# Order of the first loads and of two VectorE forks in a fused attention and feed-forward kernel on one core

## Chip, cores and metric

The kernel runs on one core of one Trainium2 chip. The metric is the device time of one execution in microseconds (us), median of several runs. Before the change the four runs took 618.7 to 620.2 us, median 619.73.

## What is computed

The input x has 8 sequences of 1024 tokens and 256 channels. It is normalized over the channels (layer norm without weights), and two branches are added to it. Cut to what matters:

```python
xn = layernorm(x)                                  # (8, 1024, 256)
# branch 1: a gated linear recurrence ("hawk"), 384 wide
gate = xn @ Wg.T;  u = xn @ Wi.T
y = depthwise_causal_conv(u, conv_w, 4 taps) + conv_b
ig = sigmoid(y @ lru_Wi.T + lru_bi);  rg = sigmoid(y @ lru_Wg.T + lru_bg)
alpha = exp(-8 * softplus(lam) * rg);  beta = sqrt(1 - alpha**2 + 1e-6)
h = scan(h[t] = alpha[t] * h[t-1] + beta * ig * y)
branch1 = (gelu(gate) * h) @ Wo.T
# branch 2: a feed-forward part with token shift
xr, xk = mu * xn + (1 - mu) * xn_shifted_by_one_token
branch2 = sigmoid(xr @ W_r.T) * (relu(xk @ W_k.T)**2 @ W_v.T)
out = x + branch1 + branch2
```

All values are float32.

## The kernel before, in words

One sequence of 1024 tokens is a round; there are eight rounds, named "first", "second", "middle" (five of them) and "last" in the table `PLACES`. Most products work on two row blocks, two column blocks and two halves of 512 tokens at once with seven block products in place of eight: `Group` (L457) writes the steps of such a group out. To that end GpSimd makes sums of weight blocks (`weight_sum`, L396, once per weight in the first round) and sums of tokens (`token_sum`, L794, in each round; the add itself is L803). Inside a group, ScalarE copies one bank of PSUM to another (`seed`, L491) and one to SBUF (`five`, L496), and VectorE adds them back in two places: `fork_c` (L499) and `fork_d` (L507). The products that follow a fork write into the banks that the fork reads or writes, so TensorE waits for it. The groups are u (three groups: u and the gate), k, r, v, o and l (three groups: the two LRU gates). TensorE's products stand at L415 (tokens in the free dimension) and L421 (tokens by row).

Instructions are issued in an order that is written out by hand. Every step is put into a list with a time, TensorE's steps with a running count, the others with their own; for the others the table `PLACES` overrides that time by a planned one, relative to the start of the round. The list is sorted by time (L1303) and issued, so each engine gets its instructions in that order and works through them one by one. A time in `PLACES` therefore sets an instruction's place in its engine's queue, and nothing else.

The second round's steps that matter here: `recur 1 R` is the second half of the scan of hidden block 1 (L930), `gated_state` multiplies the gate by the scanned state (L934), `decay_rest` makes 1 - alpha squared out of the square (L915), and `beta` takes the root of that on ScalarE (L918).

The head stands ahead of the list, at L1001 to L1105. SP issues the loads of x's first round, eight tiles of 128 tokens in four DMAs (L707). ScalarE issues the first half of u's weights (`w_i`, the "i" rows of tile `w_u`), the parameters (`par`) and a table load. Then SP issues the other weights (L349): `w_g` (the "g" rows of `w_u`), `w_k`, `w_r`, two halves of `w_l`, `w_v`, `w_o`. DMAs take their completion semaphores in turn out of eight; a DMA that takes one again is not issued before the DMA that had it last has landed. TensorE meanwhile makes 15 products of a zeroed tile (`busy`, L1025) that nobody reads. VectorE takes the statistics of each tile of x (L725, L729), ScalarE the deviation (L732), VectorE its inverse (L739, L740), and ScalarE and VectorE normalize a tile each (L749, L747). TensorE transposes two tiles (L1044), ScalarE copies them to `xnT` (L1057), and quarters of the first u group follow (L581). This repeats for four pairs of tiles. As soon as all of `xnT` is there, the token sums on GpSimd and the first group with sums (u1) can start; GpSimd has the weight sums of u, r and k ahead of the first token sum in its queue.

The lines that the change touches:

Of the kernel before, what the change touches and what calls it, by code (L numbers as in the profile page):

```python
# [9 lines left out]
AF = mybir.ActivationFunctionType  # L10
# [100 lines left out]
        "inverse 0 8": 25.96, "k late": 26.1, "conv_rest 0 1": 26.33, "u2 evict A 0 0": 26.78,  # L111
        "k evict C 0 1": 27.46, "u2 fork_c": 27.83, "gated_state 2": 28.63, "k evict B 1 0": 29.25,
        "recur 1 L": 30.04, "r seed": 31.03, "u2 fork_d": 31.49, "token_sum v 0": 31.49,
        "r five": 31.72, "u1 evict B 1 0": 32.4, "recur 1 R": 32.66, "normalize 0 1": 33.08,
        "token_sum v 1": 34.07, "r fork_c": 34.27, "r evict A 0 0": 34.3, "normalize 4 1": 34.34,
        "u2 evict C 0 1": 34.87, "gated_state 1": 34.95, "u2 evict B 1 0": 35.51, "conv_first 2": 36.19,
        "token_sum v 2": 36.35, "r fork_d": 36.36, "conv_rest 0 2": 37.5, "normalize 3 1": 37.52,
        "normalize 1 1": 38.22, "v seed": 38.92, "token_sum o 1": 38.98, "v five": 39.6,
# [21 lines left out]
        "l0 evict D 1 1": 72.36, "stats 2 1": 72.76, "token_sum k 1": 73.26, "decay 1": 73.3,  # L140
        "stats 5 1": 73.49, "stats 3 1": 74.22, "token_sum k 2": 74.42, "l2 seed": 74.64,
        "stats 1 1": 74.95, "l2 five": 75.33, "token_sum k 3": 75.59, "l1 fork_d": 75.68,
        "decay_square 1": 76.01, "mix r 1": 76.75, "l1 evict C 0 1": 77.36, "decay_rest 1": 78.25,
        "decay 2": 78.3, "l2 evict A 0 0": 79.64, "l2 fork_c": 80.36, "decay_square 2": 80.44,
        "decay_rest 0": 80.5, "decay_rest 2": 81.72, "l1 evict B 1 0": 82.36, "l1 evict D 1 1": 83.36,
        "l2 fork_d": 84.36, "l2 evict C 0 1": 90.66
    },
# [94 lines left out]
def kernel(  # L242
# [24 lines left out]
    nc = tc.nc  # L267
    B, S, D = x.shape
    TT = S // P
# [6 lines left out]
    def fixed(name, shape, dtype=F32):  # L276
        return const.tile([P] + shape, dtype, tag=name, name=name)


    par = fixed("par", [COLS])  # L280
# [57 lines left out]
    def take():  # L338
        return free.pop(0)

    def give(b):
        free.append(b)
# [4 lines left out]
    def load_weight(engine, name, src):  # L347
        family, first = ROWS[name]
        engine.dma_start(families[family][:, :, first * P : first * P + src.shape[2]], src)  # L349
# [356 lines left out]
    def load(s, t, n):  # L706
        nc.sync.dma_start(  # L707
            xt[:, t : t + n, :],
            x[s, t * P : (t + n) * P, :].rearrange("(t p) d -> p t d", p=P),
        )  # L710
# [8 lines left out]
    def stats(s, t, n):  # L719
        sums_of_tiles(s, t, n)  # L720
        moments(s, t, n)
# [279 lines left out]
    with tc.manual_schedule():  # L1001
# [1 line left out]
        nc.gpsimd.memset(ln_eps, LN_EPS)  # L1003
        nc.gpsimd.memset(beta_eps, BETA_EPS)
        make_identity(nc, ident)
        for t in range(0, TT, 2):
            load(0, t, 2)
            if t == 2:
                load_weight(nc.scalar, "i", w_i)
                nc.scalar.dma_start(par, params)  # L1010
                nc.scalar.preload_act_table(AF.Sqrt)
        load_weight(nc.sync, "g", w_g)
        load_weight(nc.sync, "k", w_k)
        load_weight(nc.sync, "r", w_r)
        load_weight(nc.sync, "lg", lru_wg)
# [6 lines left out]
        def busy(n):  # L1022
            for _ in range(n):
                b = take()
                nc.tensor.matmul(banks[b], warm[:, 0:P], warm, start=True, stop=True)  # L1025
                give(b)
# [40 lines left out]
                mu_rest, par[:, COL_MU_R : COL_MU_K + DC], -1.0, 1.0, ALU.mult, ALU.add  # L1067
            )

        busy(15)  # L1070
        stats(0, 0, 2)
        scales(0, 2)
        early_normalize(0)
# [42 lines left out]
        for s in range(B):  # L1116
# [118 lines left out]
            else:  # L1235
# [36 lines left out]
                L, R = HALVES  # L1272
# [90 lines left out]
```

## Time and profile before

| What | us |
|---|---|
| median of four runs | 619.73 |
| profiled execution, its own time | 619.65 |
| its span, first to last instruction | 617.9 |
| TensorE (PE) busy | 612.0 |
| VectorE (DVE) busy | 532.5 |
| ScalarE (ACT) busy | 472.9 |
| GpSimd (POOL) busy | 320.4 |
| 28 SP loads of x of 256 KB each, median from issue to landing | 5.0 |

The profile is one execution taken by the hardware profiler. Its lines give, in the timelines, start, duration, engine, source line, operation, output and inputs, shapes and count, and in brackets the idle time ahead and what ended it. A line that ends in "x2" merges two instructions in a row. A float32 product shows as two TensorE instructions. In the chain of waits a line gives start, duration and what the time went to. In the DMA view a queue's line gives packets, megabytes and the share of the sixteen DMA engines' time; q1 is SP's queue, q10 is ScalarE's. TensorE is busy in nearly all of the span, so what counts is where it stands still: little things of a few tenths of a microsecond.

### The profile page before, as it was taken

The page shows a single profiled execution, that of the slowest core. Times are in us where ns is not written, and L with a number is a line of the kernel's source. Part 1 is how long each engine was busy: PE and PEld are TensorE (multiplying, and loading weights), DVE is VectorE, ACT ScalarE, POOL GpSimd, SP SyncE. Part 2 cuts the span into 40 slices and gives each one's busy share as a digit, 9 for nine tenths or more (in the row PEclk, how much of TensorE's full clock was granted, in tenths as well). Part 3 has the DMA queues.
Part 4 walks back from the last instruction along what each step waited for, and adds up shares of the span by engine and source line. Part 5 has one row for each costly group of instructions (what it writes and reads, how often), then busy time and mean ns, then how long its engine had stood idle before and what let it go on. Part 6 is the DMA issues. An engine that isn't in the chain of part 4 may idle for free.

```text
span 617.9 us, 7488 instructions
## 1 busy us (share of the span) xinstructions
PE 612.0 (99%) x2539; PEld 369.5 (60%) x2539; DVE 532.5 (86%) x659; ACT 472.9 (77%) x671; POOL 320.4 (52%) x227
## 2 busy tenths in 40 slices
PE   9999999999999999999999999999999999999997
PEld 5475445954469544794448844497445964457466
DVE  5898799999989798898899888998888986789696
ACT  5888998568894788938889398884898749884880
POOL 4977914578044950549307492084911769427000
PEclk9999999999999999999999999999999999999999
DMA  8100600164002810039000480006500044000403
GB/s 282 60 1 10 127 0 1 31 174 69 0 1 50 197 27 0 1 77 198 0 1 1 107 166 1 1 6 154 114 0 1 14 124 69 0 0 1 69 17 119
DMA packets 35478, 35.10 MB, mean 57 GB/s; under 512 B 2800, under 2 KB 34928, under 8 KB 35440
## 3 DMA queue, kind: packets, MB, share of 16 engines
q1 hardware_dynamic: 26416, 25.63, 15.0%
q0 software_dynamic: 8320, 8.39, 9.1%
q10 hardware_dynamic: 704, 0.60, 0.3%
q8 instruction: 20, 0.33, 0.2%
q14 instruction: 18, 0.15, 0.1%
HBM read 19.94 MB, written 8.39 MB: 46 GB/s over the span
## 4 chain that ended last, share of the span: by engine, by line
PE 94%; DVE 2%; POOL 1%; DMA 1%; issue 0%; SPq 0%; DVEq 0%; POOLq 0%
PE bank L415 65%; PE bank L421 25%; PE bank L830 4%; DMA w_u<-in_w_g_dram 1%; POOL sum_u L408 1%; DVE xr L820 1%; POOL xsum L803 0%; DVE bank L499 0%; PE bank L754 0%; SPq L707 0%; DVE q L915 0%; POOL sum_k L408 0%; DVE st L725 0%; POOL sum_r L408 0%; DVE q L930 0%
## 5 line engine op out<-in xcount | busy, mean ns | idle before, releaser
L415 PE MATMUL bank<-y,w_l 128*128 128x512 f32 x288 | 138.2, 593 | 0.1
L898 DVE SCALAR_TENSOR_TENSOR y<-u,par,y 128x1024 f32<-128x1024 f32 x72 | 111.6, 1573 | 0.2
L491 ACT COPY bank<-bank 128x512 f32<-128x512 f32 x76 | 43.7, 576 | 61.3 <-PE bank L415 45.4
L415 PEld LDWEIGHTS bank<-y,w_l 128*128 128x128 f32 x288 | 52.9, 190 | 59.2 <-issue 56.9
L499 DVE TENSOR_TENSOR bank<-bank,five 128x512 f32<-128x512 f32 x76 | 52.3, 689 | 27.4 <-PE bank L415 26.0
L415 PE MATMUL bank<-ysum,sum_l 128*128 128x512 f32 x144 | 71.1, 594 | 0.2
L415 PE MATMUL bank<-xsum,sum_u 128*128 128x512 f32 x138 | 69.5, 593 | 0.8 <-POOL xsum L803 0.8
L803 POOL TENSOR_TENSOR tr<-g 128x512 f32<-128x512 f32 x12 | 22.0, 1837 | 83.7 <-ACT u L611 69.8
L803 POOL TENSOR_TENSOR ysum<-y,ysum 128x512 f32<-128x512 f32 x16 | 28.5, 1782 | 53.6 <-DVE y L898 51.1
L803 POOL TENSOR_TENSOR xsum<-ysum 128x512 f32<-128x512 f32 x12 | 16.0, 1351 | 66.0 <-PE bank L421 58.8
L496 ACT COPY five<-bank 128x512 f32<-128x512 f32 x76 | 43.6, 583 | 5.8 <-PE bank L415 3.8
L415 PEld LDWEIGHTS bank<-ysum,sum_l 128*128 128x128 f32 x144 | 26.8, 190 | 35.3 <-issue 28.7
L415 PE MATMUL bank<-xnT,w_u 128*128 128x512 f32 x92 | 47.0, 592 | 0.0
L415 PEld LDWEIGHTS bank<-xsum,sum_u 128*128 128x128 f32 x138 | 25.6, 190 | 30.8 <-issue 27.0
L623 ACT ACTIVATE tr<-bank,half_b 128x512 f32<-128x512 f32 x48 | 32.0, 679 | 14.7 <-PE bank L415 14.7
L421 PE MATMUL bank<-w_o,g 128*128 128x128 f32 x288 | 37.0, 275 | 0.0
L623 ACT ACTIVATE ti<-bank,half_b 128x512 f32<-128x512 f32 x48 | 31.5, 683 | 7.1 <-PE bank L415 6.9
L421 PEld LDWEIGHTS bank<-w_o,g 128*128 128x128 f32 x288 | 35.0, 192 | 2.9 <-issue 2.9
L749 ACT ACTIVATE xt<-xt,mv,std 128x256 f32<-128x256 f32 x60 | 33.9, 595 | 0.9 <-DVE mv L740 0.9
L922 DVE SCALAR_TENSOR_TENSOR ti<-ti,y 128x1024 f32<-128x1024 f32 (+1 forms) x25 | 29.9, 1216 | 3.9 <-ACT ti L623 3.9
L803 POOL TENSOR_TENSOR ysum<-y 128x512 f32<-128x512 f32 x16 | 20.4, 1276 | 23.8 <-DVE y L898 20.0
L925 DVE SCALAR_TENSOR_TENSOR ti<-ti,q 128x1024 f32<-128x1024 f32 (+1 forms) x25 | 31.8, 1271 | 0.7
(165 smaller groups left out, 1479.3 us busy)
## 6 DMA issues: line engine op xcount, KB each, us to landing
side<-in_x_dram POOLq DMA_DIRECT2D x8, 1024.0 KB, 9.2
xt<-in_x_dram SPq DMA_DIRECT2D x28, 256.0 KB, 5.0
xnT<-xk SPq DMA_DIRECT2D x96, 64.0 KB, 2.0
out_dram<-side SPq DMA_DIRECT2D x12, 512.0 KB, 4.9
xt<-in_x_dram SPq DMA_DIRECT2D x1, 1024.0 KB, 5.3
out_dram<-side SPq DMA_DIRECT2D x4, 256.0 KB, 2.2
out_dram<-side SPq DMA_DIRECT2D x6, 128.0 KB, 1.7
w_l<-in_lru_wg_dram SPq DMA_DIRECT2D x1, 576.0 KB, 5.8
```

What stands on the lines that cost most here:

```text
L415: nc.tensor.matmul(banks[b], weight, tokens, start=start, stop=True, skip_group_check=True)
L421: nc.tensor.matmul(banks[b][:, p], tokens[:, p], weight, start=start and j == 0, stop=True, skip_group_check=True,)
L491: nc.scalar.copy(banks[bank["B"]], banks[bank["A"]])
L496: nc.scalar.copy(self.five, banks[bank["C"]])
L499: nc.vector.tensor_tensor(banks[bank["C"]], banks[bank["B"]], self.five, ALU.add)
L623: nc.scalar.activation(dst[:, m, HALVES[h]], src, AF.Tanh, bias=half_b[:, b + m : b + m + 1], scale=0.5)
L749: nc.scalar.activation(xa, xa, AF.Identity, bias=m, scale=r)
L803: nc.gpsimd.tensor_tensor(dst[o], a, b, ALU.subtract)
L830: nc.tensor.matmul(banks[b][:, j * D : (j + 1) * D], lhs[:, c, (t + j) * P : (t + j + 1) * P], families[w][:, c, :], start=(j == 0 and c = ...
L898: nc.vector.scalar_tensor_tensor(y[:, m, :], u[:, m, k : k + S], column(COL_CONV_W + k * HC + m), y[:, m, :], ALU.mult, ALU.add,)
L922: nc.vector.scalar_tensor_tensor(ti[:, m, p], ti[:, m, p], 1.0, y[:, m, p], ALU.add, ALU.mult)
L925: nc.vector.scalar_tensor_tensor(ti[:, m, p], ti[:, m, p], 0.5, q[:, m, p], ALU.mult, ALU.mult)
```

## The change

It has two parts. In the head, the first two tiles of x are loaded by two DMAs of one tile each in place of one DMA of two; all of u's weights are issued by ScalarE (`w_i`, then `w_g`), ahead of `par` and the table load, while SP goes on from x to `w_k`; and TensorE makes ten warm-up products in place of 15. With one DMA more and the turn of the semaphores changed, SP's issue of `w_k` is now the one that waits for `w_i`; `w_r` waits for the first tile of x.

In the second round two steps change their place in VectorE's queue: `r fork_c` now stands ahead of `recur 1 R`, and `l2 fork_c` ahead of `decay_rest 1`. On the other engines the second round is issued as before.

```diff
 "second" in PLACES:
-        "r five": 31.72, "u1 evict B 1 0": 32.4, "recur 1 R": 32.66, "normalize 0 1": 33.08,
-        "token_sum v 1": 34.07, "r fork_c": 34.27, "r evict A 0 0": 34.3, "normalize 4 1": 34.34,
+        "r five": 31.72, "u1 evict B 1 0": 32.4, "r fork_c": 32.6, "recur 1 R": 32.66,
+        "normalize 0 1": 33.08, "token_sum v 1": 34.07, "r evict A 0 0": 34.3, "normalize 4 1": 34.34,
...
-        "decay_square 1": 76.01, "mix r 1": 76.75, "l1 evict C 0 1": 77.36, "decay_rest 1": 78.25,
-        "decay 2": 78.3, "l2 evict A 0 0": 79.64, "l2 fork_c": 80.36, "decay_square 2": 80.44,
+        "decay_square 1": 76.01, "mix r 1": 76.75, "l1 evict C 0 1": 77.36, "decay 2": 78.3,
+        "l2 evict A 0 0": 79.64, "l2 fork_c": 80.36, "decay_square 2": 80.44, "decay_rest 1": 80.45,
...
-        for t in range(0, TT, 2):
+        load(0, 0, 1)
+        load(0, 1, 1)
+        load_weight(nc.scalar, "i", w_i)
+        for t in range(2, TT, 2):
             load(0, t, 2)
-            if t == 2:
-                load_weight(nc.scalar, "i", w_i)
-                nc.scalar.dma_start(par, params)
-                nc.scalar.preload_act_table(AF.Sqrt)
-        load_weight(nc.sync, "g", w_g)
+        load_weight(nc.scalar, "g", w_g)
+        nc.scalar.dma_start(par, params)
+        nc.scalar.preload_act_table(AF.Sqrt)
         load_weight(nc.sync, "k", w_k)
...
-        busy(15)
+        busy(10)
```

## The prediction

> **What bounds the kernel now.** Three views, in this order. First the page's chain of work that ended last: 94% of the span is TensorE, so a change counts only where TensorE waits. Then the same chain for the first 30 us, and TensorE's timeline, to find where it waits: in the head, and at two places of the second round (101 to 152 us). From 150 us on the chain is TensorE alone until the last us.
>
> The chain of the head:
> ```profile
> 2.75 5.62 DMA w_u<-in_w_g_dram
> ...
> 8.52 2.98 POOL sum_u L408 x3
> ...
> 11.56 1.00 POOL sum_u L408
> ...
> 15.52 2.27 POOL xsum L803
> ...
> 17.84 12.28 PE bank L415 x28
> ```
> The second half of u's weights lands at 8.37, POOL then makes eleven weight sums one after another and only behind them the first token sum (L803), and TensorE waits for that. The timeline there (start, duration, engine):
> ```profile
> 13.52 0.59 ACT L1057 COPY xnT<-bank 128x512 f32<-128x512 f32 x1 [0.19 <-PE bank L1044]
> ...
> 15.99 1.02 PE L415 MATMUL bank<-xnT,w_u 128*128 128x512 f32 x2
> ...
> 17.84 1.13 PE L415 MATMUL bank<-xsum,sum_u 128*128 128x512 f32 x2 [0.82 <-POOL xsum L803]
> ```
> A 512-column product is two passes 0.43 apart (12.28 us / 28), so TensorE was free at 15.99 + 0.86 = 16.85 and stood still for **0.99 us**. The second bound lies close beneath: the last quarter of x is in xnT at 14.11, and TensorE works from there without a pause until 16.85, that is 2.74 us after it.
>
> VectorE at the start of the head:
> ```profile
> 3.32 0.75 DVE L725 BATCH_NORM_STATS2 st<-xt 128x6 f32<-128x256 f32 x2 [2.20 <-DMA xt<-in_x_dram]
> ...
> 5.78 0.75 DVE L725 BATCH_NORM_STATS2 st<-xt 128x6 f32<-128x256 f32 x2 [0.25 <-DMA xt<-in_x_dram]
> ...
> 9.61 1.01 DVE L747 TENSOR_SCALAR xt<-xt,std,mv 128x256 f32<-128x256 f32 x1
> ```
> Both first loads of x are waited for; they are the start of everything.
>
> **Part 1, the head.** *What it gains.* The second half of u's weights is issued by ScalarE behind the first, not by SP behind all of x. Bytes issued ahead of its end fall from 1806 KB (x, w_i, par, itself) to about 1024 KB (half of x's first pair each side of w_i, itself). At the 0.36 MB/us that the windows from 2 to 6 us show, that is 2.2 us sooner: 8.37 becomes 6.2. POOL's sums (6.9 us, 8.5 to 15.5) then end by 13.4, and the first token sum waits only for xnT. Alone it takes 1.27 (the later ones), so the 0.99 us goes: **-0.99**. Late next is xnT itself, 2.74 us ahead of the product.
>
> *What it costs.* Does x go first? The DMA view of 3.0 to 3.6 us answers with one queue:
> ```profile
> q10 hardware_dynamic: 132, 0.20, 95.1%
> ```
> That is ScalarE's queue; SP's moved nothing, though the second load of x had been issued at 1.23. So w_i (issued at 0.73 like the first load) ran as a block between the first and the second load of x. In the changed kernel the first load is one tile of 128 KB, then comes w_i (384 KB), then the second tile, then w_g (384 KB), then tiles 2 and 3. Every load of x after the first tile has 384 KB more ahead of it: 0.39 MB / 0.36 = 1.1 us, less under 0.1 for the shorter first issue, so **1.05 us later**. Tile 1: 3.3 to 4.4; tiles 2 and 3: 5.78 to 6.83; the rest alike. Tile 0 gains some 0.3 us and gives nothing, since both tiles' statistics end in one instruction each for std and scale.
>
> Tiles 2 and 3 then meet POOL. In before, their scale and normalization (L740, L747) took 0.16 and 0.41 at 7.5, just before POOL began at 8.52; for the next two tiles, beside POOL, they took 0.54 and 1.01, and each ended within 0.2 us of the end of a POOL sum. With POOL busy from 6.3 and this pair there at about 8.6, it pays the same: 0.38 + 0.60 = 0.98. The later pairs add nothing: the copies to xnT (L1057) start at 9.04, 11.28, 13.52, 2.24 apart, and a quarter of products plus four transposes plus the copy on TensorE and ScalarE fill that. So xnT is complete 1.05 + 0.98 = **2.03 later**, 16.14, and the product starts at 16.14 + 2.74 = 18.88 in place of 17.84: **+1.04 net**. Bounds: without the meeting with POOL +0.06; with x not delayed -0.99 (the first rival); with another 0.5 us, should the slow first packets hit twice, +1.5. I take the upper middle, by the rows that show VectorE held in all four cases where POOL ran.
>
> The Trainium skill ("Trainium Kernel Development and Optimization", Key Constraints) says that DMAs from several engines' queues run on the same DMA engines and interleave, and that issuing from several saves issue time alone. The view of 3.0 to 3.6 us shows no interleaving inside a transfer. If there were, 512 KB of x would have as much of u's weights beside it, 1024 KB in place of 1280: tiles 2 and 3 would be 0.36 us late, not 1.05, and the head +0.35.
>
> *The other head edits.* Ten warm-up passes: fifteen ran 1.18 to 5.99, 0.43 apart at first and about 0.2 from 4.1 on; ten end near 4.9. The first transposes (5.82) move to 6.5 with tile 1, so TensorE is idle for 1.6 us; nothing waits for it then, so 0 (second rival otherwise). ScalarE issues one DMA more (0.64) ahead of its table load (1.28), which ends at 4.0; its first work stood at 4.39 and goes later. Par's own load is needed at 12.64 and landed by 6. SP: w_k's issue now waits for w_i (as w_r's did, 1.0 us); with 2318 KB up to w_r's end both land between 9 and 10, and POOL wants them from 10.4. If they came 1 us later the token sum would still be ready, since xnT rules. The next x load (13.56, 5.3 to land) slips 2 us; its statistics began at 18.89, ahead of a VectorE wait of 1.93: covered.
>
> **Part 2, the second round.** TensorE's and VectorE's rows:
> ```profile
> 106.68 1.02 PE L415 MATMUL bank<-xsum,w_u 128*128 128x512 f32 x2
> 107.80 2.05 PE L421 MATMUL bank<-sum_r,xr 128*128 128x128 f32 x16
> ...
> 125.70 1.13 PE L421 MATMUL bank<-w_o,tr 128*128 128x128 f32 x8
> ...
> 148.21 1.88 PE L415 MATMUL bank<-y,w_l 128*128 128x512 f32 x4
> 150.23 1.13 PE L415 MATMUL bank<-ysum,sum_l 128*128 128x512 f32 x2
> ```
> ```profile
> 104.84 2.31 DVE L930 TENSOR_TENSOR_SCAN q<-tr,q,ti 128x512 f32<-128x512 f32 x1
> 107.08 0.67 DVE L499 TENSOR_TENSOR bank<-bank,five 128x512 f32<-128x512 f32 x1
> ...
> 124.93 0.69 DVE L507 TENSOR_TENSOR bank<-bank,five 128x512 f32<-128x512 f32 x1
> ...
> 147.82 1.75 DVE L915 TENSOR_SCALAR q<-q 128x1024 f32<-128x1024 f32 x1
> 149.49 0.69 DVE L499 TENSOR_TENSOR bank<-bank,five 128x512 f32<-128x512 f32 x1
> ```
> *r's fork.* TensorE could go on at 106.68 + 0.86 = 107.54 and waits for the fork until 107.80. Put ahead of the scan, the fork waits for its product (104.89 + 1.06 = 105.95), runs to 106.67, and TensorE gains 0.26. But the scan is queued behind it. It starts at 106.6 instead of 104.84, where it had stood 1.07 us beside POOL's token sum; the next token sum (106.03, 1.27 alone) holds it until 107.3, it ends at 108.4, and the scaled state behind it (1.22) at 109.5 against 109.30. VectorE is 0.2 us late. From there to the fork at 124.93 it has one gap of 0.1, and TensorE's 125.70 starts 0.08 after that fork. So 0.26 is returned and about **+0.1** stays. Bounds: -0.26 if VectorE catches up; +1.0 if all of its new idle time (104.93 to 106.0) is passed on.
>
> *l2's fork.* TensorE could go on at 148.21 + 4 x 0.43 = 149.93 and starts at 150.23. The fork's product ended at 147.52 and VectorE's work ahead at 147.89, so the fork ends by 148.5: **-0.30**. The scaling behind it mostly waited for POOL's sum (146.77 to 149.03) and still ends near 149.6; its reader, a square root, comes at 152.13. Bounds -0.30 and 0. TensorE has no gap behind it, so this stays.
>
> **Sum.** +1.04 + 0.1 - 0.30 = +0.84. The profiled execution took 619.65 (span 617.9 and 1.75 around it), 0.08 under the median of 619.73. Forecast 619.65 + 0.84 = **620.5**. With the bounds of the parts the case reaches from 619.15 (+0.06 - 0.26 - 0.30) to 621.85 (+1.5 + 1.0 - 0.30).
>
> **Rivals.** *x keeps its place (faster).* If the second tile's packets are ready before w_i's and queues take turns, or if w_i's slow start (its first two packets took 704 and 798 ns) does not come again, x is not later. For it: w_i's issue takes 0.64 and the tile's less than the 0.44 of a pair. Against: the empty SP queue above. Then -0.99 - 0.30 with -0.26 to +0.1: 618.1 to 618.5, say **618.3**; 617.8 if tile 0's 0.3 us counts, and 619.3 if tiles 2 and 3, now at 7.5 with POOL busy from 6.3, still pay their 0.98.
> *The clock (slower).* TensorE's passes came closer only 2.9 us after the first (1.18 to 4.1). If five passes fewer and 1.6 us idle from 4.9 let the clock fall back before the quarters, 2.9 us of work must again run at half speed: 1.4 us more, **621.9**. It has happened if the passes of 256 columns near 8 us, 0.22 apart in before (eight in 1.97), stand 0.43 apart. Against: the idle 0.99 us at 17 us left the passes behind it 0.43 apart as before.
> By the Trainium skill ("TensorE: Matmul & The Clock Gate", What's actually happening) only an idle window of about 3.4 us brings the slow clock back; by that, this rival costs nothing.
> *The new first-in-line is w_r.* If SP's later issue brings w_r after 12 us, POOL is no sooner and the 0.99 stays; with the x delay it is still xnT that rules, so the time is the forecast's.
>
> **Numbers.** Forecast 0.64, x in place 0.20, clock 0.16. A change within 0.2% (1.24 us) is about what measurement can tell from none. Of the forecast 0.47 lies within and 0.17 above; of the first rival 0.15 beyond on the fast side and 0.05 within; the clock is slower whole. Faster 0.15, same 0.52, slower 0.33. The range 618.2 to 621.8 leaves out about half of each rival.
>
> **What would show it.** Right: no packet of x between w_i's first and last; tile 1's statistics near 4.4, tiles 2 and 3 near 6.8; L747 of that pair near 1 us; the first xsum product near 18.9, waiting for no POOL; TensorE without a gap at 107.5 and 149.9, with one at 125.7. Wrong: tile 1 by 3.5 and the xsum product before 17; or products of the head at half speed.

## Result and profile after

The changed kernel takes 620.66 us (median of 38 runs, 620.05 to 623.47); the kernel before, on the same chip, 619.82 (59 runs, 618.7 to 620.75). By the medians that is 0.84 us (0.14%) more; the ratio of the means, in which the long runs of the changed kernel count, is 1.002, 95% interval 1.0015 to 1.0025: small, but clear of no change. The runs of the kernel before crowd near 619 and near 620.3, 30 at 619.82 or less and 29 at 620.01 or more, so its median lies at the edge between two groups and moves from chip to chip. The profiled execution of the changed kernel took 620.41 with a span of 618.6. The forecast of 620.5 holds. But some of its terms were mis-sized, one edit that was costed at nothing is worth something, and the gain of 0.99 us that it counts on stands in the one profile that it was read from.

The chain of waits of the changed kernel, first 31 us (start, duration, what):
```profile
1.63 6.10 DMA xt<-in_x_dram
7.73 0.02 issue
7.76 0.75 DVE st L725 x2
...
9.69 1.06 DVE xt L747
...
15.83 2.67 PE bank L581 x12
18.50 12.88 PE bank L415 x30
```
The weights and GpSimd are gone from it. It now runs from the second pair of x, through VectorE, to the quarters of products, and from there without a gap into the first group. GpSimd and TensorE in the timeline of the changed kernel:
```profile
7.69 1.95 POOL L408 TENSOR_TENSOR sum_u<-w_u 128x384 f32<-128x384 f32 x2 [6.25 <-DMA w_u<-in_w_g_dram]
...
16.53 1.30 POOL L803 TENSOR_TENSOR xsum<-xnT 128x512 f32<-128x512 f32 x1 [1.86 <-ACT xnT L1058]
```
```profile
18.34 1.02 PE L415 MATMUL bank<-xnT,w_u 128*128 128x512 f32 x2
19.20 1.02 PE L415 MATMUL bank<-xsum,sum_u 128*128 128x512 f32 x2
```
GpSimd finished its sums early and waited 1.86 us for `xnT`; the product with token sums follows its predecessor by 0.86 us, without a stall, but at 19.20 in place of 17.84. VectorE of the changed kernel shows why:
```profile
4.72 0.43 DVE L725 BATCH_NORM_STATS2 st<-xt 128x6 f32<-128x256 f32 x1 [1.37 <-DMA xt<-in_x_dram]
...
7.76 0.75 DVE L725 BATCH_NORM_STATS2 st<-xt 128x6 f32<-128x256 f32 x2 [1.16 <-DMA xt<-in_x_dram]
...
9.46 0.19 DVE L740 SCALAR_TENSOR_TENSOR mv<-mv,std 128x2 f32<-128x2 f32 x1
9.69 1.05 DVE L747 TENSOR_SCALAR xt<-xt,std,mv 128x256 f32<-128x256 f32 x1
```
Tiles 2 and 3 are 1.98 us late (7.76 against 5.78), not 1.05, and their normalization meets GpSimd's sums (1.05 in place of 0.41).

The second round, TensorE and then VectorE of the changed kernel:
```profile
107.79 1.02 PE L415 MATMUL bank<-xsum,w_u 128*128 128x512 f32 x2
108.65 1.95 PE L421 MATMUL bank<-sum_r,xr 128*128 128x128 f32 x16
...
125.59 1.02 PE L415 MATMUL bank<-ysum,sum_l 128*128 128x512 f32 x2
126.93 1.16 PE L421 MATMUL bank<-w_o,tr 128*128 128x128 f32 x8 [0.32 <-DVE bank L507]
...
149.47 1.88 PE L415 MATMUL bank<-y,w_l 128*128 128x512 f32 x4
151.18 1.02 PE L415 MATMUL bank<-ysum,sum_l 128*128 128x512 f32 x2
```
```profile
107.17 0.70 DVE L499 TENSOR_TENSOR bank<-bank,five 128x512 f32<-128x512 f32 x1 [1.13 <-PE bank L421]
107.78 1.73 DVE L930 TENSOR_TENSOR_SCAN q<-tr,q,ti 128x512 f32<-128x512 f32 x1
109.54 1.23 DVE L934 TENSOR_TENSOR g<-g,q 128x1024 f32<-128x1024 f32 x1
...
126.19 0.69 DVE L507 TENSOR_TENSOR bank<-bank,five 128x512 f32<-128x512 f32 x1
```
At 108.65 and 151.18 the product behind the fork starts 0.86 and 1.71 us (two and four passes of 0.43) behind its predecessor's start: both stalls are gone. At 126.93 a new one stands, 1.34 us behind a start that needs 0.86. VectorE first stood idle 1.13 us ahead of the fork, and the scan queued behind it came late.

Set side by side, instruction by instruction, TensorE's weight loads of the two profiles give the balance of the whole change: the changed kernel is 1.25 us late after the head, 1.13 from 38.8 on (there the kernel before had to wait and the changed one no longer does), 0.75 after r's fork, 1.26 from 126 on, 0.84 after l2's fork, and 0.84 at the end.

### The profile page after: what moved, and what is told of

The parts are those of the page before. It is cut to its first block, busy times and chain, and to the rows that moved or that the text cites. A ratio compares the mean times of both kernels' runs of the same rounds, so it can differ in the third digit from the quotient of the medians.

```text
span 618.6 us, 7480 instructions
## 1 busy us (share of the span) xinstructions
PE 611.2 (99%) x2534; PEld 369.5 (60%) x2534; DVE 529.2 (86%) x659; ACT 472.8 (76%) x671; POOL 319.5 (52%) x227
## 4 chain that ended last, share of the span: by engine, by line
PE 95%; DVE 3%; DMA 1%; issue 1%; SPq 0%; DVEq 0%
PE bank L415 66%; PE bank L421 22%; PE bank L830 4%; DVE y L898 1%; PE bank L581 1%; DMA xt<-in_x_dram 1%; DVE xk L780 0%; DVE bank L499 0%; PE bank L754 0%; DVE q L930 0%; PE bank L1045 0%; DVE st L725 0%; DVE xt L747 0%; SPq L707 0%; DVE side L507 0%
```

## Experiments

Every run shared its chip with runs of the kernel before; the ratio is to those, and "before" is their median. "Late" is how late TensorE's last loads are in the profile, against the profile of before, set side by side as above. "Falls" counts the executions in which the granted clock went back to half in the course of the kernel. It is read from the mean granted clock that is on record for each execution: a stretch of 3.4 us at half gives 0.997 (the profile of head_g_on_sp), one of 6.8 us gives 0.995 (that of head_only), and no execution of the kernel before beside these runs is below 0.999.

| Run | median us (from to) | before | ratio, 95% interval | late in the profile, us | falls |
|---|---|---|---|---|---|
| head_only | 620.90 (620.02 to 624.41) | 620.15 | 1.0023, 1.0009 to 1.0037 | 3.78 | 7 of 12 |
| second_only | 620.00 (618.80 to 620.24) | 620.15 | 0.9997, 0.9989 to 1.0006 | 0.49 | 0 of 11 |
| l2_only | 619.58 (618.56 to 620.35) | 620.15 | 0.9989, 0.9980 to 0.9997 | 0.41 | 0 of 11 |
| pool_order | 619.27 (618.38 to 620.52) | 620.15 | 0.9990, 0.9980 to 1.0000 | 0.60 | 0 of 12 |
| before_busy10 | 619.21 (618.91 to 619.68) | 619.88 | 0.9987, 0.9978 to 0.9995 | 0.06 | 0 of 11 |
| head_g_on_sp | 620.75 (620.49 to 621.46) | 619.88 | 1.0015, 1.0007 to 1.0024 | 1.74 | 6 of 11 |
| head_pair | 621.19 (619.84 to 622.64) | 619.88 | 1.0020, 1.0009 to 1.0031 | 1.00 | 5 of 12 |
| head_busy15 | 621.12 (620.35 to 623.18) | 619.88 | 1.0020, 1.0009 to 1.0031 | 0.82 | 2 of 11 |
| head_fill | 620.87 (620.13 to 623.61) | 620.19 | 1.0022, 1.0011 to 1.0034 | 1.50 | 1 of 12 |
| best | 618.48 (618.28 to 620.08) | 620.19 | 0.9984, 0.9975 to 0.9994 | -1.32 | 0 of 12 |
| best_busy2 | 620.18 (619.37 to 620.68) | 620.19 | 1.0004, 0.9995 to 1.0012 | 0.65 | 0 of 11 |
| l2_busy10 | 618.57 (618.38 to 619.46) | 620.29 | 0.9979, 0.9970 to 0.9989 | -0.65 | 0 of 10 |

The changed kernel itself has 15 falls in 39 executions on record. With the loads of the kernel before there is none in any run: all falls belong to the changed loads.

### The two parts alone

head_only has the edits from L1003 on, second_only those in `PLACES`; l2_only moves `l2 fork_c` alone.

> Only the head of the change, the second round in the old order. If the weights' blocks ahead of x are what costs: about 1.1 us slower than before (the shift of TensorE's products behind 39 us in the changed kernel's trace was 1.13), tiles 2 and 3 of x landing near 7.7, and gaps of TensorE at 107.5 and 150 as in before. If the loss came from the second round: no difference from before.

> Only the two forks moved, the head as before. By the traces: r's fork gains 0.36 at 107.5 and loses 0.51 at 125.7, l2's fork gains 0.42 at 150, together 0.27 us faster. Rival: the loss at 125.7 was a result of the later head; then 0.8 us faster.

> Only l2's fork ahead of the scaling. Theory: 0.42 us faster, TensorE without a gap at 150. Rival, the scaling that is pushed back makes ScalarE's roots late and the time is given back in the next round: no difference.

The cost is in the head: 620.90 beside 620.15, +0.75. The second round alone shows in its profile the same steps as in the whole change: 0.38 gained at r's fork, 0.52 lost at 126, 0.41 gained at l2's fork (0.41 in l2_only too). So the rival, that the loss at 126 comes from the later head, is out. In the times, second_only can't be told from the kernel before; l2_only is faster. By the medians, without r's move it is 0.42 better (619.58 against 620.00); the two intervals overlap.

The profile of head_only fell on one of its long executions (623.33) and shows the second rival at work. Its table of stretches gives length, busy time and instructions of each engine, then the granted clock:
```profile
5.00:8.50 3.50, 1.66 (x9) 0.74 (x8) 1.43 (x7) 1.48 (x3) 0.69 (x1) 1.00 1.03 305
8.50:15.40 6.90, 5.66 (x15) 3.94 (x16) 6.12 (x23) 2.46 (x6) 6.20 (x11) 0.51 0.86 318
15.40:20.00 4.60, 4.60 (x26) 3.76 (x25) 0.00 (x0) 3.35 (x6) 0.71 (x1) 1.00 0.03 10
```
and its timeline
```profile
12.69 3.22 PE L581 MATMUL bank<-xnT,w_u 128*128 128x256 f32 x8
...
16.18 1.97 PE L581 MATMUL bank<-xnT,w_u 128*128 128x256 f32 x8
```
TensorE was busy 1.66 of 3.50 us, then the clock was granted half for 6.8 us, and eight products took 3.22 in place of 1.97. This is a fall of the clock. The chain of waits of this run reaches the first group at 21.25, 2.75 later than that of the changed kernel: 0.57 because tiles 2 and 3 came at 8.33, 0.63 because L740 and L747 were held longer, and 1.55 from the clock (three transposes 0.90 in place of 0.55, eight products 3.01 in place of 1.81). The rival had priced it at 1.4. Over 621.3 us lie 10 of the changed kernel's 38 runs and none of the kernel before's 59. But the time is no sure sign of a fall. The four executions of the changed kernel at 0.995 took 622.58 to 623.47; of its eleven at 0.997, nine took 620.22 to 621.28; and four of the ten above 621.3 show no fall at all. Why those are long is open.

### The stall behind GpSimd, taken away without touching the loads

```diff
-        "early weight_sum k 2 False": 6.13, "early weight_sum k 1 False": 6.5, "early load 0 8": 6.86,
-        "early_put 3": 6.86, "early weight_sum r 1 False": 6.87, "early weight_sum k 3 False": 7.18,
-        "early mix_before k 0": 7.48, "early token_sum x 0": 7.5, "early weight_sum r 3 False": 8.66,
+        "early weight_sum k 2 False": 6.13, "early weight_sum k 1 False": 7.61, "early load 0 8": 6.86,
+        "early_put 3": 6.86, "early weight_sum r 1 False": 10.6, "early weight_sum k 3 False": 7.62,
+        "early mix_before k 0": 7.48, "early token_sum x 0": 7.5, "early weight_sum r 3 False": 10.61,
```
(and `l2 fork_c` moved)

> Loads as before and l2's fork moved; in GpSimd's queue of the first round two weight sums of k (rows 1 and 3) go behind the first token sum and two of r (1 and 3) behind the second. If what held TensorE at 17 us was only the number of weight sums ahead of the first token sum: the first xsum product near 16.9 in place of 17.84 and 1.0 + 0.42 = 1.4 us faster. Rival: the wait only moves to a later token sum or to k's products (24.8 us): 0.4 us faster.

By the medians it is 0.88 faster than the kernel before and 0.31 faster than l2_only, with overlapping intervals: the 1.4 of its theory is not there. Its profile was 0.60 late, not early (product with token sums at 18.78), because of something the prediction did not have: the time at which the warm-up products come closer. They stand 0.43 us apart until 4.1 us in the profile of before, but until 5.8 to 6.6 in those of second_only, l2_only and pool_order. There, fifteen of them outlast the first normalized tiles. The chain of second_only:
```profile
1.18 5.76 PE bank L1025 x15
6.94 0.45 PE bank L1044 x4
```
The transposes (L1044) start at 6.9, behind the warm-up, in place of 5.8. So in this the profile of before was a lucky execution. The next run tests whether the upper group of the kernel before's times, near 620.4, comes from here.

### Ten warm-up products alone

```diff
-        busy(15)
+        busy(10)
```

> The kernel before with ten warm-up products in place of fifteen, nothing else. Theory (the spread of the kernel before comes from the clock's rise): where the clock rises late, at 5.7 to 6.6 us in the runs so far, fifteen passes 0.43 us apart last until 6 or later and hold the first transposes, which are ready near 5.8; ten end by 5.6. The profile shows the first transposes at 5.8 to 6.0 and the first product of token sums near 17.8, with the stall behind GpSimd, whenever the clock rises; the times keep their floor of 618.7 but lose the upper group around 620.5, so the median goes from 620.1 to about 619.3, ratio 0.9985 to 0.999. Rival 1 (five passes fewer let the clock fall back): matmuls of the head twice as far apart for several us, median 621 or more in a good part of the executions. Rival 2 (the spread is from elsewhere): median and spread as before, ratio 1.0000 within 0.0003.

In the times, as the theory had it: 619.21 beside 619.88, no run above 619.68, and no fall of the clock, so the first rival is out. In its profile the clock rises only at 7 us; its chain:
```profile
1.18 4.45 PE bank L1025 x10
5.63 0.41 issue
6.04 1.10 PE bank L1044 x4
```
The ten have ended 0.41 us before the transposes, which run at half speed but start at 6.04.

One thing the theory expected is missing: the stall behind GpSimd. The product with token sums starts at 17.93, 2.74 us behind `xnT`, without a wait. GpSimd's and VectorE's lines show what differs, first in the kernel before, then here:
```profile
15.37 3.49 DVE L820 SCALAR_TENSOR_TENSOR xk<-xnT,par,xk 128x1024 f32<-128x1024 f32 x2 [2.25 <-ACT xk L814]
15.47 2.31 POOL L803 TENSOR_TENSOR xsum<-xnT 128x512 f32<-128x512 f32 x1
```
```profile
15.56 1.30 POOL L803 TENSOR_TENSOR xsum<-xnT 128x512 f32<-128x512 f32 x1
16.46 2.88 DVE L820 SCALAR_TENSOR_TENSOR xk<-xnT,par,xk 128x1024 f32<-128x1024 f32 x2 [2.83 <-ACT xk L814]
```
GpSimd came to its token sum as late as in the kernel before (15.56 against 15.47). But there VectorE had begun to mix `xk` (L820) 0.10 us earlier, and the sum took 2.31 in place of 1.30. With 1.30 it would have ended at 16.77, ahead of the 16.85 at which TensorE was free. Of the five profiles with the loads and GpSimd's order of the kernel before (before, second_only, l2_only, before_busy10, l2_busy10) only that one has the stall; in the other four the sum took 1.29 or 1.30, and the product came 2.74 behind `xnT`. The second token sum fits: 1.27 in the kernel before, behind the end of L820 (19.14), and 2.25 in before_busy10, beside it (18.22). So the 0.99 us is the outcome of a race, in one profiled execution of five.

### Which edit of the head costs the time

head_g_on_sp takes `w_g` back to SP's queue behind x; head_pair loads the first two tiles in one DMA; head_busy15 has fifteen warm-up products; head_fill has 13, and six in place of two behind the first transposes. All have the rest of the changed head and the second round of before.

Against the changed head, head_g_on_sp and head_pair:

```diff
-        load_weight(nc.scalar, "g", w_g)
         nc.scalar.dma_start(par, params)
         nc.scalar.preload_act_table(AF.Sqrt)
+        load_weight(nc.sync, "g", w_g)
```
```diff
-        load(0, 0, 1)
-        load(0, 1, 1)
+        load(0, 0, 2)
```
and head_fill (head_busy15 has 15 and 2):
```diff
-        busy(10)
+        busy(13)
...
-        busy(2)
+        busy(6)
```

> The changed head without one of its parts: the second half of u's weights goes back to SP's queue, behind all of x. Single tiles and ten passes stay, the second round is that of the kernel before. Theory (that half, ahead of tiles 2 and 3, is what makes them late): their statistics, at 7.76 in the changed kernel, come back to 5.8 to 6.3, the last quarter of x is in its place by 14.3, GpSimd starts its sums at 8.4 again and the product of token sums waits for it, near 17.9. Time that of the kernel before with ten passes, 619.2 to 619.8. Rival (the first half and the splitting into single tiles make them late): statistics of tiles 2 and 3 still after 7, product after 18.5, time 620.5 or more.

> The changed head with its first two tiles in one load of 256 KB again; u's weights on ScalarE's queue and ten passes stay, the second round is that of the kernel before. Theory (the weights ahead of tiles 2 and 3 cost the time, not the split): first statistics at 3.3 for both tiles, but those of tiles 2 and 3 still at 7.4 to 7.8, product of token sums at 18.9 to 19.2, time 620.4 to 621 as with the whole changed head. Rival (the second tile behind the first weights costs it): the transposes start at 5.8 instead of 6.9, all pairs follow earlier and the product starts by 18.2, time 619.8 or less.

> The changed head with fifteen warm-up products again; loads as changed, the second round is that of the kernel before. Theory (ten passes and the gap behind them let the clock fall back in some executions): fifteen end by 6.2, ahead of the transposes at 6.9, so they hold nothing; no execution shows the clock record at 0.5 again between 8 and 16 us, values above 621.3 (about a third with ten passes) go, median 620.3 to 620.6, ratio 1.000 to 1.001. Rival (the fall comes from the thin work behind 7 us, whatever the passes): the share above 621.3 stays at about a third and the median at 620.9.

> The changed head with 13 warm-up products in place of ten and six in place of two behind the first transposes; loads as changed, the second round is that of the kernel before. Theory (the clock falls back where TensorE has too little work between 5.5 and 10 us): the fillers keep it busy until about 9, delay nothing that is waited for (the second pair's transposes come near 10.2), so no clock record at 0.5 after the rise, the values above 621.3 go and the median is 620.3 to 620.7. Rival (it falls whatever TensorE does there, or the fillers themselves hold the quarter): a third or more above 621.3, median 620.9 or later.

*head_g_on_sp* went to its rival. Tile 1, behind `w_i`, came at 5.42:
```profile
5.42 0.43 DVE L725 BATCH_NORM_STATS2 st<-xt 128x6 f32<-128x256 f32 x1 [2.15 <-DMA xt<-in_x_dram]
```
Tiles 2 and 3 followed at 7.22 without waiting for their DMA: VectorE worked the first pair off until then. The clock fell back here too, from 8.9 to 12.3. There is no stall behind GpSimd, and the time is no better. *head_pair* has the product (19.05) and the slower time of the theory, but not its mechanism:
```profile
5.75 0.75 DVE L725 BATCH_NORM_STATS2 st<-xt 128x6 f32<-128x256 f32 x2
...
8.57 0.75 DVE L725 BATCH_NORM_STATS2 st<-xt 128x6 f32<-128x256 f32 x2 [1.85 <-DMA xt<-in_x_dram]
9.24 0.15 DVE L739 RECIPROCAL std<-std 128x2 f32<-128x2 f32 x1
...
9.62 0.98 DVE L747 TENSOR_SCALAR xt<-xt,std,mv 128x256 f32<-128x256 f32 x1
```
The first pair came at 3.57, and tiles 2 and 3 at 5.75, as in the kernel before. What waits until 8.57 are tiles 4 and 5. Their statistics stand in VectorE's queue ahead of the inverse (L739) of the second pair, so that pair is normalized at 9.62, as late as in the changed kernel (9.69). The times of issue fit: `w_g` is issued at 1.41, tiles 2 and 3 at 1.23, tiles 4 and 5 at 1.72; in the changed kernel the split moves tiles 2 and 3 to 1.63, behind `w_g` at 1.40.

So either edit alone makes the head late: the single tiles make the first pair wait for `w_i`, and `w_g` on ScalarE's queue holds the x that is issued behind it. They don't add up: the second pair is normalized (L747) at 9.92 with the one, 9.62 with the other, 9.69 with both, against 7.69 in before.

*head_busy15* went to its rival in the times: 3 of 11 runs above 621.3 (ten passes: 3 of 12 in head_only). *head_pair*, where TensorE makes its second pair's transposes only at 10.27, has 6 of 12. Counted by the clock, fifteen passes do not prevent the fall (2 of 11), and ten (before_busy10, best, l2_busy10) or even two (best_busy2) do not bring it about when x comes as in the kernel before (0 of 33 and 0 of 11). Whether fifteen make it rarer, 2 of 11 against 22 of 51 with ten passes in head_only and the changed kernel, can't be told. What is left is the thin work of TensorE while it waits for x; that is argued, not shown. *head_fill* speaks for it, with 1 fall in 12, but at the same median (620.87), and its profile has tile 1 at 5.55 and is 1.50 late without a fall. How much of the tail the fillers take is open.

### Combinations

best is pool_order with ten warm-up products, best_busy2 the same with two, l2_busy10 the same as best with GpSimd's order left as before.

> The kernel before with its loads, and three edits: ten warm-up products in place of fifteen, l2's fork ahead of the scaling, and GpSimd's weight sums of k and r put behind the first two token sums in its queue. Theory (each takes away a wait of its own): ten products alone gave 618.9 to 619.7; l2's fork takes off 0.42; with the weight sums out of the way the product of token sums starts at 16.9 to 17.3 in place of 17.9, 0.6 to 1.0 less, since the last quarter of x is in its place at 14.6 to 15.2. Sum 617.6 to 618.6, median 618.1, ratio 0.997. Rival 1 (what GpSimd puts off is missed later, at r's or k's first products): the gain at 17 us is returned by 40 us, median 618.8. Rival 2 (the late clock slows the quarters of products and they take the stall's place): median 618.8 with a wide spread.

> As the run with ten warm-up products, weight sums put off and l2's fork, but with two warm-up products in place of ten. Theory (the passes are what brings the clock up before the quarters of products): with only two, the clock record rises after 7 us, the first one or two quarters run 0.43 us apart in place of 0.21, and the product of token sums starts 0.5 to 2 us later; median 618.6 to 620. Rival (the passes do nothing, the clock rises by its own time at 4 to 7 us): same time as with ten, within 0.2 us.

> The kernel before with ten warm-up products and l2's fork ahead of the scaling, GpSimd's order as before: the combination without the edit on GpSimd. In the traces that edit was worth 0.97 us (product of token sums at 16.88 in place of 17.84); by the medians the combination lies only 0.73 below ten passes alone, of which l2's fork takes 0.42. Theory (the trace's stall behind GpSimd is there in all executions): 618.48 + 0.97 = 619.45, so 619.3 to 619.6. Rival (executions without that stall are common, so that it is worth little in the median): 619.21 - 0.42 = 618.79, so 618.6 to 618.9.

best runs in 618.48 and lies below both kernels. In its profile the stall is gone:
```profile
14.22 1.30 POOL L803 TENSOR_TENSOR xsum<-xnT 128x512 f32<-128x512 f32 x1
```
```profile
16.88 1.02 PE L415 MATMUL bank<-xsum,sum_u 128*128 128x512 f32 x2
```
But l2_busy10, without that edit, takes 618.57: in the medians the edit is worth 0.09, on different chips, not the 0.67 by which the two profiles differ (-1.32 and -0.65). Its rival holds. The two profiles differ by the clock: the granted clock rose at 4.13 in best's and at 6.55 in l2_busy10's, so `xnT` was complete at 14.14 and 14.90, and in both the product started 2.74 behind it. The kernel before has runs at 618.7, which is 0.95 under its profiled one. A token sum of 1.30 in place of 2.31 would account for them, but none of them was profiled.

best_busy2 shows what the warm-up is for. With two, TensorE comes to its full rate only after 11 us, and the first quarters run at half speed:
```profile
7.80 2.07 PE L581 MATMUL bank<-xnT,w_u 128*128 128x256 f32 x4
```
against 1.13 in before. It takes 1.70 us more than with ten.

## Why the prediction was right, and where it was not

*Weights earlier, stall gone (-0.99): right against the one profile, wrong in its cause.* GpSimd began at 7.69, not 6.2, and still waited for `xnT`. The step that failed is that the eleven weight sums made TensorE wait. They ended at 15.47, in time for a token sum of 1.30; the wait was the 1.01 us by which VectorE's L820 stretched that sum in this execution. I had the 1.27 of the later sums beside the 2.27 in the chain and did not ask why they differ. Against an execution without the stall this term is nothing.

*x later by 1.05: the mechanism right, the size wrong; it was 1.98.* The step that failed is the rate: 0.36 MB/us, read from before between 2 and 6 us, was taken over for stretches with other transfers in them. Two stretches of the DMA view, 3.5 to 5.5 us, of the kernel before and then of the changed one (packets, MB, share of the sixteen engines' time):
```profile
DMA packets 827, 0.72 MB, mean 361 GB/s; under 512 B 188, under 2 KB 827, under 8 KB 827
...
q1 hardware_dynamic: 563, 0.55, 77.9%
q10 hardware_dynamic: 264, 0.17, 28.3%
```
```profile
DMA packets 422, 0.48 MB, mean 242 GB/s; under 512 B 51, under 2 KB 422, under 8 KB 422
...
q10 hardware_dynamic: 235, 0.31, 67.2%
q1 hardware_dynamic: 187, 0.18, 28.5%
```
The changed kernel moved 0.24 MB less; at 0.36 MB/us that is 0.67 us of the 0.93 missing. Fourteen packets of u's weights took over 0.3 us each, up to 1.03, most of them near 4.2 us, where `w_g` begins; in before two did (the 704 and 798 ns of the prediction). "should the slow first packets hit twice" was the bound of that term, and it is what happened. Why they are slow there is open. How late each tile is changes from execution to execution: tile 1 came at 4.72, 4.87, 5.42 and 5.55, tiles 2 and 3 at 7.60 to 8.33 in the heads with single tiles and all of u's weights on ScalarE's queue.

*The meeting with GpSimd (+0.98): half right.* L747 was held (1.05, +0.64), L740 was not (0.19 in place of 0.16). In the other heads L740 of this pair took 0.61 and 0.70 (head_g_on_sp, head_only) or 0.16 and 0.18 (head_pair, head_busy15, head_fill), so it depends on where beside GpSimd's sums it falls. Here 0.67, not 0.98, and only 0.37 of it reaches `xnT`, which is complete 8.70 behind the start of these statistics in place of 8.33. The two errors partly cancel: `xnT` complete at 16.46 (forecast 16.14). The 2.74 us from there to the product held exactly: 19.20. The head cost 1.25 at first, 1.13 from 38.8 on (forecast 1.04).

*Ten warm-up products (0): wrong in the usual execution.* I read their end from one profile, with the clock up at 4.1 us. Over the runs it is worth -0.67 (before_busy10). In the changed head the gain is not seen (head_only 620.90, head_busy15 621.12), as its transposes wait for tile 1 until 6.9 anyway.

*r's fork (+0.1): right.* 0.38 gained (forecast 0.26), 0.51 returned at 126: +0.13. *l2's fork (-0.30): right in sign, -0.42.* Both gains came out 0.12 larger than the gaps read: a product that has waited shows some 0.11 us longer (150.23, 1.13 against 1.02), and that goes with the stall.

*The sum:* +1.13 + 0.13 - 0.42 = +0.84, as forecast. That it meets the forecast to the hundredth is luck: the errors of two terms partly cancel, and the balance is drawn against one execution of the kernel before that had both an early clock and the stall. That the medians differ by 0.84 too is luck as well, since that of before lies between its two groups; the means differ by 1.24.

*Rivals.* x did not keep its place: tile 1 at 4.72, tiles 2 and 3 at 7.76. The clock's fall is real, in 15 of 39 executions rather than as the whole outcome, and not for the reason given (five passes fewer): it comes with fifteen too, and never with ten where x is not late. The rule quoted there, that only an idle window brings the slow clock back, doesn't hold as I used it (the section names an idle window; the "only" is mine): in head_only TensorE was busy for 1.66 of the 3.50 us before the fall. The Trainium skill ("TensorE: Matmul & The Clock Gate", What's actually happening) also says that the window of about 3.4 us runs freely, so that the time of the rise varies from run to run. With that the runs agree (the clock rose at 4.0 to 7.1 us wherever there were ten passes or more, wider than the half microsecond each way that the page names), and I should have read it against the fifteen passes.

The other rule weighed there, interleaving, is half borne out: in 3.5 to 5.5 us both queues move, in 3.0 to 3.6 us of before one of them alone did. The sign set against it, no packet of x between `w_i`'s first and last, was not met: from 3.0 to 3.6 us of the changed kernel SP's queue moved 50 packets beside ScalarE's 101.

The third rival cost nothing: GpSimd's first sum of `w_r` started at 11.64 without a wait.

## What to carry to other kernels

A single profile fixes one phase of whatever varies from run to run: before costing an edit at nothing, look for what would change if the clock rose two microseconds later. Before taking a stall for a gain, ask why the instruction that is waited for took as long as it did; one that takes 2.31 us here and 1.30 elsewhere may be a race. Weights issued earlier on another queue are paid by the loads that the head waits for, and at the start of a kernel at more than their bytes. When a load comes late, look in the waiting engine's queue for whose work stands behind it: in head_pair the pair that was late had its own data in time. Where two stalls lie close together, what removing one is worth has to be measured as a median, not read from one trace.

## What the runs showed of the hardware that was not expected

- TensorE came to its full rate at 4.1 us in one execution and at 7 us in another of nearly the same program (before, before_busy10): 3 us of spread. With fifteen passes the first transposes then started as late as 7.10 in place of 5.82 (l2_only), and TensorE's work behind 39 us was up to 0.85 late.
- The granted clock fell to half for 6.8 us (8.5 to 15.4, head_only) and 3.4 us (8.9 to 12.3, head_g_on_sp) with TensorE partly busy ahead of it (1.66 of 3.50 us and 1.27 of 3.40).
- A token sum of 128x512 on GpSimd took 2.31 us where VectorE's L820 had started 0.10 us before it (before), and 1.30 where it had started 0.90 us ahead of L820 (before_busy10).
- Packets of 1536 bytes that took up to 1.03 us near the start of the second weight DMA, while the others took less than 0.3 us; from 3.5 to 5.5 us the total rate was 242 GB/s, against 361 in the kernel before.
